# Products with two weight matrices in a graph-transformer kernel: from four matmuls a row tile to Strassen's scheme on pairs of row tiles

## Chip, cores and metric

The kernel runs on one core of one Trainium2 chip. The metric is the device time of one execution in microseconds (us). Times of several runs are given by their median. The profile comes from one further execution, whose own time is given with it.

## What is computed

A layer of graph attention and a layer of graph convolution, in float32, over N = 3327 nodes with D = 512 features. The adjacency `adj` is an N × N matrix; bq and bk are zero vectors in the inputs. Cut to what matters:

```python
h = relu(layernorm(x))
q, k, v = h @ Wq.T + bq, h @ Wk.T + bk, h @ Wv.T + bv
a = q @ k.T / sqrt(D) + adj + adj
x = x + softmax(a) @ v
h = relu(layernorm(x))
A2 = adj + eye(N)
d = diagonal(A2) ** -0.5
temp = A2 @ h @ W.T
x = x + relu((d[:, None] * A2 * d[None, :]) @ temp)
```

Since the rows of the softmax sum to one, softmax(a) @ v is (softmax(a) @ h) @ Wv.T + bv, and the kernel computes it in that order. In the same way temp is (A2 @ h) @ W.T.

## The kernel before

The nodes are padded to 26 row tiles of 128. The work has three stages.

Stage 1 (lines 311 to 374) loads x tile by tile, normalises it (`norm`), makes h with ScalarE, stores h in the buffer `rowd[0]`, and transposes h on TensorE. It also makes M from Wq and Wk and multiplies the transposed h by it. These products use Strassen's scheme in Winograd's form: seven products of half-size blocks in place of eight, with sums and differences of blocks ahead and behind (`Chain`, `four_differences`).

Stage 2 (lines 379 to 563) makes the scores, their exponentials and the sums over the rows, and stores the exponentials in the buffers `pd`.

Stage 3 (lines 574 to 1001) is where the change lies. It has three groups, g = 0, 1 and 2: exponentials times h, A2 times the new h, and A2 times temp. Each group is one big product in Strassen's scheme at two levels. At the outer level there are seven products r, in the order p5, p1, p6, p7, p2, p3, p4. Each is made for two strips of columns, s = 0 (448 columns for each matmul) and s = 1 (384 columns), and each strip in seven steps: t = 0 to 5, and a last, short step t = None. So a group has 98 steps, and `number_of(g, r, s, t)` gives a step's number. In what follows (6,0,1) is the step of product number 6, strip 0, t = 1; a leading 1 in (1,0,0,2) stands for the next group.

A step t = 0 to 5 has seven matmuls (L772), one for each inner product, into seven PSUM banks that keep summing over the strip's steps. The short step has four (L764). The eighth bank, named p8, belongs to the short step's last matmul and, between the short steps, to the products with the weights. For each step:

- `load` issues the DMA of the left side on SyncE's queue, three steps ahead (L751).
- `sums` makes the left side's four sums with three VectorE additions (L170 to L172), two steps ahead.
- `Right.load` and `Right.make` (L715, L731) load the right side's rows and make its eight blocks with VectorE, two to five steps ahead.
- After a short step, `gather` copies p1 out with ScalarE (L806) and combines the eight banks with eight VectorE additions (L807 to L816). `settle` (L795 to L802) then combines outer products. The results are the transposed strips `cts`.
- `Job` (L824 to L842) adds two stored matrices with VectorE and stores the sum with a DMA from GpSimd's queue (POOL in the profile).

When some rows of a group's result are complete in `cts`, the products with the weights begin. They are attached to later steps with `at(k, ...)`, and run after that step's own matmuls. `times_weights` (L844) takes a tile of 128 rows and multiplies it by Wv (g = 0) or W1 (g = 1): four matmuls of 512 columns (L848) into bank p8. For g = 0, `attend_load` (L853) loads the tile of x a step earlier, on ScalarE's queue. `attend` (L857) scales the product by the reciprocal of the softmax sum and adds x (VectorE, L860), adds bv (VectorE, L861), stores the result in `x1d`, and starts the norm. `attended` (L865), a step later, makes the new h with ScalarE (L867) and stores it in `rowd[1]`. For g = 1, `temp` (L872) reads the bank with ScalarE, scaled (L876), and stores the tile in `rowd[2]`. The next group's right sides are loaded from these rows.

The order within each engine is set by hand. `in_order` (L120, L993) keeps VectorE, TensorE, GpSimd, ScalarE and SyncE in the order in which the code writes their instructions. `run(k)` (L973) writes one step: loads, matmuls, gather, sums of step k + 2, settle, and then what `between` holds for k, in the order in which `at` put it there.

Of the kernel before, what the change touches and what calls it, by code (L numbers as in the profile page):

```python
# [15 lines left out]
P = 128  # L16
# [20 lines left out]
PAIRS = 6  # L37
# [7 lines left out]
def graph_layers_kernel(  # L45
# [117 lines left out]
    totd = dram.tile([1, NP], F32, name="totd")  # L163
    x1d = [dram.tile([P, D], F32, name=f"x1d{i}") for i in range(NT)]
# [3 lines left out]
    def four_sums(o, g):  # L168

        nc.vector.tensor_add(o[:, 0:2], g[:, 0:4:3], g[:, 1:2].to_broadcast([P, 2, g.shape[-1]]))  # L170
        nc.vector.tensor_add(o[:, 2], o[:, 1], g[:, 0])  # L171
        nc.vector.tensor_add(o[:, 3], o[:, 2], g[:, 2])  # L172
# [116 lines left out]
    nc.sync.dma_start(bq_sb, bq)  # L289
    M = blocks(range(4, 8), "M")  # L290
# [3 lines left out]
    zero = half(12, [P, P], "zero")  # L294
# [16 lines left out]
    def h_transposed(k):  # L311

        a, n = PACKS[k]
        for _, i in (o for o in order if o[0] == k):
# [9 lines left out]
            if i < HALF:  # L324
                nc.scalar.copy(hp[k][:, 0:2, :, w], pt.rearrange("p (a c) e -> p a c e", a=2))
            else:
                nc.scalar.copy(hp[k][:, 2, :, w], pt[:, 2:4])
                nc.vector.tensor_add(hp[k][:, 3, :, w], hp[k][:, 2, :, w], pt[:, 0:2])
                nc.vector.tensor_add(hp[k][:, 5, :, w], hp[k][:, 0, :, w], pt[:, 0:2])
        nc.vector.tensor_add(hp[k][:, 4], hp[k][:, 3], hp[k][:, 0])  # L330
# [280 lines left out]
    rs = const.tile([P, NT], F32, name="rs")  # L611

    def weights(src):

        w = [half(k, [P, 2, D], "w") for k in (12, 13)]
        for c in range(DC):
            nc.sync.dma_start(w[c // 2][:, c % 2], src[c * P : (c + 1) * P])
        return [w[c // 2][:, c % 2] for c in range(DC)]
# [4 lines left out]
    bvs = []  # L623

    def prepare():
        wv_w1.append(weights(wvT))
        bvs.append(half(11, [P, D], "bv_sb"))
        nc.sync.dma_start(bvs[0], bass.AP(tensor=bv.tensor, offset=bv.offset, ap=[[0, P], [1, D]]))
# [4 lines left out]
    def prepared():  # L633
        nc.vector.reciprocal(rs, tot)
        nc.vector.tensor_scalar(dg, dg, 1.0, None, op0=ALU.add)
        nc.gpsimd.tensor_tensor(sd, dg, mh, op=ALU.pow)

    wv_w1 = []

    def other_weights():  # L640
        wv_w1.append(weights(w1T))
# [17 lines left out]
    r_ring = ring(*((half, k) for k in (4, 5, 6, 7)))  # L659
# [11 lines left out]
    job_ring = ring(*spare[2:], (half, 14))  # L671
    h_ring = ring(*spare[:2])
    ts_ring = ring(*spare[:3])
# [25 lines left out]
    class Right:  # L699
# [31 lines left out]
        def make(self):  # L731
            own, r = self.own, self.r
            if r == "p5":
                nc.vector.tensor_sub(own, self.two[:, :, 0:E], self.two[:, :, E:D])
            if r == "p6":
                nc.vector.tensor_add(own, own, self.two[:, :, 0:E])
                nc.vector.tensor_sub(own, own, self.two[:, :, E:D])
                nc.gpsimd.dma_start(self.t2[:, 0 : 2 * self.n], self.b[:, 0 : 2 * self.n])
            if r in ("p7", "p4"):
                nc.vector.tensor_sub(own, own, self.one)  # L740
            if self.n == 2:
                for _ in four_differences([self.b[:, k] for k in range(8)]):
                    pass

    class Step:
# [8 lines left out]
        def sums(self):  # L754
# [3 lines left out]
            four_sums(self.o, self.a.rearrange("p k y w -> p (k y) w"))  # L758

        def multiply(self, ps):  # L760
            a, b, w = self.a, self.right.b, Q[self.s]
            if self.t is None:
                for k, (y, z) in enumerate(((0, 0), (0, 1), (1, 0), (1, 1))):
                    nc.tensor.matmul(ps[("p2", "p3", "p4", "p8")[k]][:, :w], b[:, z], a[:, 0, y],  # L764
                                     start=k == 3, stop=True)
                return
            o = self.o
            for r, i, m in (
# [3 lines left out]
                nc.tensor.matmul(ps[r][:, :w], b[:, i], m, start=self.t == 0,  # L772
                                 stop=self.t == PAIRS - 1 and r in ("p1", "p5", "p6", "p7"))
# [70 lines left out]
    def times_weights(i, w):  # L844
        s, y, k = where(i)
        ps = bank(ROLE["p8"], "p8")
        for d in range(DC):
            nc.tensor.matmul(ps, cts[s][y][d][:, k * P : (k + 1) * P], w[d], start=d == 0, stop=d == DC - 1)  # L848
        return ps

    xts = {}

    def attend_load(i):  # L853
# [525 lines left out]
```

## Time and profile before

| what | value |
|---|---|
| median of three runs | 2237.49 us (2237.46 to 2239.75) |
| the profiled execution | 2234.41 us |
| its span in the profile | 2232.6 us, so 1.8 us lie around it |
| mean granted clock of TensorE | 0.993 |
| TensorE (PE) busy | 2183.9 us |
| VectorE (DVE) busy | 1622.8 us |
| ScalarE (ACT) busy | 230.8 us |
| GpSimd (POOL) busy | 357.0 us |
| products with Wv and W1, L848 | 125.4 us (x272) and 67.6 us (x144) |

In the profile PE is TensorE's matmuls and PEld its weight loads, which overlap them. A line such as `L848 PE MATMUL p<-w,ct 128*128 128x512 f32 x272 | 125.4, 601` is a group of instructions: line 848, the engine, the operation, output and inputs with their shapes, the number of records, and after the bar the busy time in us and the mean length of one in ns. What follows a second bar is the idle time of the engine just before them and what ended most of it. Matmuls overlap, so the mean length of one (601 ns here) is more than the distance from one to the next; busy time counts overlaps once. A float32 matmul leaves two records: `x416` for L848, in its two groups, are 208 matmuls, four for each of 26 tiles in two groups g. A wait line gives the instruction that waited, the one that released it, the total in us, how often, and the longest.

### The profile page before, as it was taken

The numbers are of one execution on the slowest core, as the hardware profiler recorded it, in microseconds if no ns is written. First come the engines' busy times: TensorE is split into PE (matmuls) and PEld (weight loads), VectorE is DVE, ScalarE is ACT, GpSimd is POOL, SyncE is SP. The second block draws the span as 40 slices with busy tenths as digits, with TensorE's granted clock in tenths as the row PEclk, the third lists the DMA queues.
The fourth block names the chain that finished last, engine by engine and source line by source line (L and its number), as shares of the span: only waits on it lengthen the run. The fifth ranks groups of instructions, "written<-read, shape, count | busy, mean of one in ns | idle before, by whom it ended". The sixth has DMA issues, their size and how long they took to land. (4 is left out here: it accounts for less than half of the span.)

```text
span 2232.6 us, 21006 instructions
## 1 busy us (share of the span) xinstructions
PE 2183.9 (98%) x6268; PEld 1166.9 (52%) x6268; DVE 1622.8 (73%) x3096; ACT 230.8 (10%) x336; POOL 357.0 (16%) x555
## 2 busy tenths in 40 slices
PE   9999999999999999999999999999999999999996
PEld 6555555455555555555444555555554555555554
DVE  6369888788777788877777778886543457777775
ACT  5321121112110000000010000000000000000011
POOL 4223333333321000001222110000000000000001
PEclk9999999999999999999999999999999999999998
DMA  7568888888969898888787899876636458766684
GB/s 249 203 218 301 297 293 286 303 285 303 355 205 335 318 362 295 283 297 275 254 299 238 300 341 354 279 277 199 223 119 203 141 176 291 247 196 190 212 304 151
DMA packets 246412, 583.68 MB, mean 261 GB/s; under 512 B 34770, under 2 KB 105904, under 8 KB 246288
## 3 DMA queue, kind: packets, MB, share of 16 engines
q1 hardware_dynamic: 191824, 398.89, 53.9%
q0 software_dynamic: 45104, 167.88, 19.9%
q10 hardware_dynamic: 9360, 15.47, 2.2%
q8 instruction: 52, 0.85, 0.2%
q14 instruction: 72, 0.59, 0.1%
HBM read 414.28 MB, written 167.85 MB: 261 GB/s over the span
## 5 line engine op out<-in xcount | busy, mean ns | idle before, releaser
L772 PE MATMUL p<-part,b 128*128 128x448 f32 (+1 forms) x3528 | 1253.2, 513 | 5.8 <-DVE part L171 5.2
L772 PEld LDWEIGHTS p<-part,b 128*128 128x128 f32 x3528 | 666.7, 190 | 572.6 <-issue 297.9
L170 DVE TENSOR_TENSOR part<-part 128x896 f32<-128x896 f32 (+1 forms) x252 | 256.6, 1018 | 84.9 <-PE p L772 40.1
L449 PE MATMUL Y<-qt,hp 128*128 128x448 f32 (+1 forms) x832 | 309.3, 514 | 4.6 <-DVE g L453 3.6
L449 PEld LDWEIGHTS Y<-qt,hp 128*128 128x128 f32 x832 | 157.1, 190 | 140.7 <-issue 72.3
L449 PE MATMUL Z<-qt,hp 128*128 128x384 f32 (+1 forms) x416 | 162.6, 513 | 0.0
L172 DVE TENSOR_TENSOR part<-part,part 128x448 f32<-128x448 f32 (+1 forms) x219 | 129.4, 591 | 16.7 <-PE p L772 0.9
L171 DVE TENSOR_TENSOR part<-part,part 128x448 f32<-128x448 f32 (+1 forms) x219 | 129.4, 591 | 7.3
L848 PE MATMUL p<-w,ct 128*128 128x512 f32 x272 | 125.4, 601 | 5.7 <-DVE part L860 4.0
L764 PE MATMUL p<-part,b 128*128 128x448 f32 (+1 forms) x336 | 124.2, 513 | 0.0
L449 PEld LDWEIGHTS Z<-qt,hp 128*128 128x128 f32 x416 | 78.8, 190 | 67.4 <-issue 36.4
L453 DVE SCALAR_TENSOR_TENSOR g<-g,Y 128x384 f32<-128x384 f32 (+1 forms) x156 | 91.3, 585 | 26.9 <-PE Y L449 25.4
L842 POOL DMA_DIRECT2D sum<-job x52 | 28.4, 547 | 486.8 <-DVE job L839 267.7
L807 DVE TENSOR_TENSOR part<-p,part 128x384 f32<-128x384 f32 (+1 forms) x33 | 19.3, 585 | 105.7 <-ACT part L806 57.5
L764 PEld LDWEIGHTS p<-part,b 128*128 128x128 f32 x336 | 63.5, 190 | 53.7 <-issue 32.8
L848 PEld LDWEIGHTS p<-w,ct 128*128 128x128 f32 x272 | 51.9, 192 | 67.5 <-issue 51.9
L806 ACT COPY part<-p 128x384 f32<-128x384 f32 (+1 forms) x33 | 16.5, 499 | 667.4 <-PE p L772 667.4
L449 PE MATMUL X<-qt,hp 128*128 128x384 f32 (+1 forms) x208 | 81.1, 513 | 0.0
L456 ACT ACTIVATE g<-g 128x768 f32<-128x768 f32 (+1 forms) x48 | 43.0, 896 | 353.8 <-DVE g L453 291.9
L848 PE MATMUL p<-w,part 128*128 128x512 f32 x144 | 67.6, 606 | 5.5 <-DVE ct L816 5.5
L441 POOL DMA_DIRECT2D sum<-o x52 | 36.8, 709 | 222.2 <-DVE o L435 155.7
L89 POOL DMA_DIRECT2D out_dram<-r x34 | 18.4, 542 | 302.9 <-DVE r L897 275.0
(160 smaller groups left out, 1877.8 us busy)
## 6 DMA issues: line engine op xcount, KB each, us to landing
part<-sum SPq DMA_DIRECT2D x104, 448.0 KB, 4.9
part<-p SPq DMA_DIRECT2D x91, 448.0 KB, 6.6
part<-sum SPq DMA_DIRECT2D x104, 384.0 KB, 3.5
part<-p SPq DMA_DIRECT2D x91, 384.0 KB, 4.0
part<-in_adjT_dram SPq DMA_DIRECT2D x78, 448.0 KB, 4.9
b<-row SPq DMA_DIRECT2D x234, 128.0 KB, 4.9
part<-in_adjT_dram SPq DMA_DIRECT2D x78, 384.0 KB, 3.7
g<-in_adjT_dram SPq DMA_DIRECT2D x52, 448.0 KB, 4.7
```

What stands on the lines that cost most here:

```text
L170: nc.vector.tensor_add(o[:, 0:2], g[:, 0:4:3], g[:, 1:2].to_broadcast([P, 2, g.shape[-1]]))
L171: nc.vector.tensor_add(o[:, 2], o[:, 1], g[:, 0])
L172: nc.vector.tensor_add(o[:, 3], o[:, 2], g[:, 2])
L441: nc.gpsimd.dma_start(self.to(sumd)[:, 0:2], self.o)
L449: nc.tensor.matmul(ps[:, :wd], h_of(self.t, name, k), qt[B[name]][:, k], start=start and k == 0, stop=k == 1, skip_group_check=True)
L453: nc.vector.scalar_tensor_tensor(a[n], a[n], 2.0, ps[:, :wd], op0=ALU.mult, op1=ALU.add if sign > 0 else ALU.subtract)
L456: nc.scalar.activation(g[1], g[1], AF.Exp, **({"bias": pad} if self.t == HALF - 1 else {}))
L764: nc.tensor.matmul(ps[("p2", "p3", "p4", "p8")[k]][:, :w], b[:, z], a[:, 0, y], start=k == 3, stop=True)
L772: nc.tensor.matmul(ps[r][:, :w], b[:, i], m, start=self.t == 0, stop=self.t == PAIRS - 1 and r in ("p1", "p5", "p6", "p7"))
L807: nc.vector.tensor_sub(c22, p["p6"], c11)
L842: nc.gpsimd.dma_start(sumd[self.s][self.j][:, 2 + self.k], self.a)
L848: nc.tensor.matmul(ps, cts[s][y][d][:, k * P : (k + 1) * P], w[d], start=d == 0, stop=d == DC - 1)
```

## The change

The products with Wv and W1 are now made for pairs of row tiles, 13 pairs in each of the two groups g. A pair is a matrix of 2 × 2 blocks of 128 rows by 256 columns, and the weight matrix is 2 × 2 blocks of 256 × 256. `Weighted` makes the seven products of Strassen's scheme in the order p2, m1, p5, p6, p3, p7, p4 (`PARTS`). Each part has two matmuls of 256 columns, into one or the other half of bank p8, where successive parts are partly summed. After each part its half is read, scaled, by ScalarE (p2, p5, p6, p4) or by VectorE, which adds to what is there (m1, p3, p7).

A pair belongs to one step k. In that step a part is followed by one of the step's seven matmuls (by two between p7 and p4). After each of these, two operations of `beside` are written: the sums of step k + 2 and then all that `between` holds for k. For this, `four_sums`, `make` and `multiply` became generators. Eight VectorE additions of 128 × 128 blocks, which a pair needs, are written at the end of step k − 1 (`coming`).

For g = 0, x + bv is made in stage 1 with one VectorE addition for each tile, and stored by a DMA from GpSimd's queue in the new buffer `xbd`. At the end of step k an accumulating DMA adds it to the tile in place of the load of x and of the two additions (`close`). The store in `x1d` and the norm follow in step k + 1, and the relu and the store in `rowd[1]` in step k + 2. The weights are loaded as blocks into four half slots, and their four differences and a change of sign are made in later steps. Some buffers move: the ring for right-side rows has three slots and not four, the ring for jobs has four other slots, bv lies in slot 12 from stage 1 on.

Line numbers of the changed kernel are those of its own file: the block additions are at L879, the parts' matmuls at L889, ScalarE's read at L899, VectorE's at L901, the accumulating DMA at L917.

The diff, cut to its core:

```diff
@@ -327,6 +330,8 @@
                 nc.scalar.copy(hp[k][:, 2, :, w], pt[:, 2:4])
                 nc.vector.tensor_add(hp[k][:, 3, :, w], hp[k][:, 2, :, w], pt[:, 0:2])
                 nc.vector.tensor_add(hp[k][:, 5, :, w], hp[k][:, 0, :, w], pt[:, 0:2])
+            nc.vector.tensor_add(xt, xt, bv_sb)
+            nc.gpsimd.dma_start(xbd[i], xt)
         nc.vector.tensor_add(hp[k][:, 4], hp[k][:, 3], hp[k][:, 0])
         nc.vector.tensor_add(hp[k][:, 6], hp[k][:, 1], hp[k][:, 4])
...
@@ -609,36 +614,45 @@
     def weights(src):
 
-        w = [half(k, [P, 2, D], "w") for k in (12, 13)]
-        for c in range(DC):
-            nc.sync.dma_start(w[c // 2][:, c % 2], src[c * P : (c + 1) * P])
-        return [w[c // 2][:, c % 2] for c in range(DC)]
+        if not W:
+            b11, b21, b22, t1, t2, t3, t4, b12 = blocks((7, 12, 13, 14), "w")
+            W.extend((b11, b12, b21, b22, t1, t2, t3, t4))
+        for z in range(2):
+            for y in range(2):
+                block = src[z * E : (z + 1) * E, y * E : (y + 1) * E]
+                nc.sync.dma_start(W[2 * z + y], block.rearrange("(c p) e -> p c e", p=P))
+        differences.append(four_differences(W))
+
+    differences = []
+
+    def difference():
+        next(differences[-1])
+
+    def turn_sign():
+        nc.scalar.mul(W[0], W[0], -1.0)
 
...
     b_ring = ring(*((half, k) for k in (0, 1, 2, 3, 8, 9, 10)))
-    r_ring = ring(*((half, k) for k in (4, 5, 6, 7)))
+    r_ring = ring(*((half, k) for k in (4, 5, 6)))
...
     spare = [(mid, k) for k in range(10, 15)]
-    job_ring = ring(*spare[2:], (half, 14))
-    h_ring = ring(*spare[:2])
-    ts_ring = ring(*spare[:3])
+    job_ring = ring(*spare[1:])
+    ts_ring = ring(*spare)
...
-    def times_weights(i, w):
-        s, y, k = where(i)
-        ps = bank(ROLE["p8"], "p8")
-        for d in range(DC):
-            nc.tensor.matmul(ps, cts[s][y][d][:, k * P : (k + 1) * P], w[d], start=d == 0, stop=d == DC - 1)
-        return ps
-    xts = {}
-    def attend_load(i):
-        xts[i] = view(2, 1).rearrange("p a w -> p (a w)")[:, len(xts) % 3 * D :][:, :D]
-        nc.scalar.dma_start(xts[i], x[i * P : (i + 1) * P])
-    def attend(i):
-        xt, ps = xts[i], times_weights(i, wv_w1[0])
-        nc.vector.scalar_tensor_tensor(xt, ps, rs[:, i : i + 1], xt, op0=ALU.mult, op1=ALU.add)
-        nc.vector.tensor_add(xt, xt, bvs[0])
-        nc.gpsimd.dma_start(x1d[i], xt)
-        normed[i] = norm(xt)
-    def attended(i):
-        h1 = h_ring([P, D], "h1")
-        nc.scalar.activation(h1, xts[i], AF.Relu, bias=normed[i][1](), scale=normed[i][0])
-        nc.gpsimd.dma_start(rowd[1][i], h1)
-    normed = {}
-    def temp(i):
-        ps = times_weights(i, wv_w1[1])
-        ts = ts_ring([P, D], "ts")
-        nc.scalar.mul(ts, ps, sd[:, i : i + 1])
-        nc.gpsimd.dma_start(rowd[2][i], ts)
+    PARTS = (("p2", 1, True, 0, 1), ("m1", 0, True, 0, -1), ("p5", 1, False, 3, -1), ("p6", 0, False, 1, -1),
+             ("p3", 1, False, 1, 1), ("p7", 0, False, 3, 1), ("p4", 0, False, 2, 1))
+    class Weighted:
+        def __init__(self, *its):
+            self.its = its
+        def sums(self):
+            a11, a12, a21, a22 = self.blocks = [
+                [cts[s][y][2 * z + c][:, k * P : (k + 1) * P] for c in range(2)]
+                for s, y, k in map(where, self.its) for z in range(2)
+            ]
+            self.o = half(11, [P, 4, 2, P], "rows")
+            for k, x, y in ((1, a21, a22), (2, None, a11), (3, None, a12), (0, a11, a21)):
+                for c in range(2):
+                    yield nc.vector.tensor_add(self.o[:, k, c], self.o[:, {2: 1, 3: 2}[k], c] if x is None else x[c], y[c])
+        def start(self):
+            self.ps = bank(ROLE["p8"], "pw").rearrange("p (k e) -> p k e", k=2)
+        def multiply(self, j):
+            name, k, new, _, _ = PARTS[j]
+            left = {"m1": 0, "p2": 1, "p4": 3}.get(name)
+            for c in range(2):
+                a = self.o[:, {"p7": 0, "p5": 1, "p6": 2, "p3": 3}[name], c] if left is None else self.blocks[left][c]
+                nc.tensor.matmul(self.ps[:, k], a, W[B[name]][:, c], start=new and c == 0, stop=c == 1,
+                                 skip_group_check=True)
+        def read(self, j):
+            name, k, _, n, sign = PARTS[j]
+            i = self.its[n // 2]
+            to, ps = self.to[n // 2][:, n % 2 * E : (n % 2 + 1) * E], self.ps[:, k]
+            scale = self.scales[sign][:, i : i + 1]
+            if name in ("p2", "p5", "p6", "p4"):
+                nc.scalar.mul(to, ps, scale)
+            else:
+                nc.vector.scalar_tensor_tensor(to, ps, scale, to, op0=ALU.mult, op1=ALU.add)
+    class Attended(Weighted):
+        scales = {1: rs, -1: nrs}
+        places = itertools.cycle(((0, 1), (2, 3)))
+        def start(self):
+            super().start()
+            v = view(2, 1).rearrange("p a w -> p (a w)")
+            places = [*(v[:, n * D : (n + 1) * D] for n in range(3)), W[1].rearrange("p a e -> p (a e)")]
+            self.to = [places[n] for n in next(Attended.places)]
+        def close(self):
+            for i, xt in zip(self.its, self.to):
+                nc.gpsimd.dma_start(xt, xbd[i], accum_op=ALU.add)
+        def norm(self):
+            self.normed = []
+            for i, xt in zip(self.its, self.to):
+                nc.gpsimd.dma_start(x1d[i], xt)
+                self.normed.append(norm(xt))
+        def then(self):
+            for i, xt, (rstd, bias) in zip(self.its, self.to, self.normed):
+                nc.scalar.activation(xt, xt, AF.Relu, bias=bias(), scale=rstd)
+                nc.gpsimd.dma_start(rowd[1][i], xt)
+    class Temp(Weighted):
+        scales = {1: sd, -1: nsd}
+        def start(self):
+            super().start()
+            self.to = [ts_ring([P, D], "ts") for _ in self.its]
+        def close(self):
+            for i, ts in zip(self.its, self.to):
+                nc.gpsimd.dma_start(rowd[2][i], ts)
...
+    weighted, coming = {}, {}
+    def rows(k, i, *z):
+        at(k - 1, finish_load, i, *z)
+        at(k, finish, i, *z)
+    def pair(g, k, *its):
+        w = weighted[k] = (Attended, Temp)[g](*its)
+        coming.setdefault(k - 1, []).append((w.sums, ()))
         if g == 0:
-            at(k - 1, attend_load, i)
-            at(k, attend, i)
-            at(k + 1, attended, i)
-        elif g == 1:
-            at(k, temp, i)
-        else:
-            at(k - 1, finish_load, i, *z)
-            at(k, finish, i, *z)
-    for g in range(3):
-        for t, i in {2: 0, 3: 1, 4: 2, 5: 3}.items():
-            rows(g, number_of(g, 5, 1, t), i)
-        for t, i in enumerate((4, 5, 6, 14, 15, 16)):
-            rows(g, number_of(g, 6, 0, t), i)
-        for t, its in {1: (7,), 2: (8, 9), 3: (10,), 4: (11, 12), 5: (13,)}.items():
-            for i in its:
-                rows(g, number_of(g, 6, 1, t), i)
-        if g < 2:
-            for k, i in enumerate((*range(20, 26), *range(17, 20))):
-                rows(g, number_of(g + 1, 0, 0, 0) + 2 * k, i)
+            at(k + 1, w.norm)
+            at(k + 2, w.then)
+    for g in range(2):
+        for (n, r, s, t), its in {
+            (0, 5, 1, 2): (0, 1), (0, 5, 1, 4): (2, 3),
+            (0, 6, 0, 1): (4, 5), (0, 6, 0, 3): (6, 14), (0, 6, 0, 5): (15, 16),
+            (0, 6, 1, 2): (7, 8), (0, 6, 1, 3): (9, 10), (0, 6, 1, 5): (11, 12),
+            (1, 0, 0, 2): (13, 19), (1, 0, 0, 4): (20, 21),
+            (1, 0, 1, 1): (22, 23), (1, 0, 1, 3): (24, 25), (1, 0, 1, 5): (17, 18),
+        }.items():
+            pair(g, number_of(g + n, r, s, t), *its)
...
-    at(number_of(1, 1, 0, 4), other_weights)
+    at(number_of(1, 1, 0, 4), weights, w1T)
+    for k in (number_of(0, 1, 0, 0), number_of(1, 2, 0, 0)):
+        for n in range(4):
+            at(k + n, difference)
+        at(k + 4, turn_sign)
...
+    def flow(tasks):
+        for what, args in tasks:
+            yield from what(*args) or (None,)
     def run(k):
         step = steps[k]
@@ -980,14 +1062,32 @@
             set_up()
         if step.t is None:
             banks_of["p8"] = bank(ROLE["p8"], "p8")
-        step.multiply(banks_of)
-        rest = gather(cts[step.s], step.r, step.s, banks_of) if step.t is None else None
-        if k + 2 < len(steps):
-            steps[k + 2].sums()
-        if rest:
-            rest()
-        for what, args in between.get(k, ()):
-            what(*args)
+        w = weighted.get(k)
+        sums = steps[k + 2].sums() if k + 2 < len(steps) else iter(())
+        others = between.get(k, ())
+        if w is None:
+            for _ in step.multiply(banks_of):
+                pass
+            rest = gather(cts[step.s], step.r, step.s, banks_of) if step.t is None else None
+            for _ in sums:
+                pass
+            if rest:
+                rest()
+            for _ in flow((*others, *coming.get(k, ()))):
+                pass
+            return
+        beside = itertools.chain(sums, flow(others))
+        w.start()
+        for j, _ in enumerate(itertools.chain((None,), step.multiply(banks_of))):
+            if j != len(PARTS) - 1:
+                w.multiply(min(j, len(PARTS) - 1))
+                w.read(min(j, len(PARTS) - 1))
+            for _ in itertools.islice(beside, 2):
+                pass
+        for _ in itertools.chain(beside, flow(coming.get(k, ()))):
+            pass
+        w.close()
```

## The prediction

> **What bounds the kernel now.** I read the page's busy times first, then TensorE's waits, then the chain of work that ended last, then the timeline and the windows around the products with Wv and W1.
>
> ```profile
> span 2232.6 us, 21006 instructions
> ...
> PE 2183.9 (98%) x6268; PEld 1166.9 (52%) x6268; DVE 1622.8 (73%) x3096; ACT 230.8 (10%) x336; POOL 357.0 (16%) x555
> ```
>
> TensorE is busy for 98% of the span; VectorE has 610 us free in the mean, ScalarE almost everything. So streaming taken from TensorE is time, and every wait put on TensorE is time.
>
> ```profile
> PE p L848 <- DVE ct L816: 5.5, 2, 4.8
> ...
> PE p L848 <- DVE part L860: 4.0, 3, 2.3
> ...
> PE p L848 <- ACT ts L876: 1.7, 2, 0.8
> ```
>
> The old products (L848) wait 11.2 us in seven places (total, times, longest). From the chain (start, duration), long undisturbed stretches of step matmuls:
>
> ```profile
> 1301.39 27.09 PE p L772 x84
> ...
> 1331.06 31.57 PE p L772 x84
> ```
>
> A matmul leaves two records. 27.09/84 = 0.3225 us a record at 384 columns, 31.57/84 = 0.3758 at 448: 0.833 ns a column and 2.5 ns. That gives 0.429 at 512 and 0.2158 at 256: 0.858 us for an old 512-column matmul, 0.432 for a new 256-column one, 0.645 and 0.752 for a step matmul of strip 1 and 0.
>
> **What the Trainium skill says.** "TensorE: Matmul & The Clock Gate", Back-to-back issue gap: N columns take N/2.4 GHz and about 2.5 ns; the two lengths above agree, with two passes a record. The same page, Part 1: an idle window of about 3.4 us halves TensorE's clock, and about 3.4 us of work restores it; the windows below agree. "PSUM — Partial Sum Buffer", Terms: two engines may not be in one bank at once; in the trace a product that reuses its bank starts only after the read. "DMA: Bandwidth & Descriptors", SWDGE vs HWDGE: an accumulating DMA can be issued by GpSimd only; this trace has none.
>
> **The change, part by part.**
>
> *Streaming.* A pair of row tiles took 8 × 0.858 = 6.87 us and takes 7 × 2 × 0.432 = 6.04. 26 pairs in two groups: **−21.4 us**. A weight load lasts 190 ns (page, L772), under the 216 ns of a record, so loads stay hidden.
>
> *Old waits.* The 11.2 us go, with about 0.1 of refill each: −12. A long wait costs more than itself (timeline, then windows whose first column after the interval is length and whose column before the last two is the clock):
>
> ```profile
> 1063.97 5.36 PE L848 MATMUL p<-w,ct 128*128 128x512 f32 x8 [2.31 <-DVE part L860]
> ```
> ```profile
> 1064.00:1065.00 1.00, 1.00 (x2) 0.48 (x3) 0.97 (x2) 0.00 (x0) 0.06 (x1) 0.50 1.02 410
> ...
> 1068.00:1069.00 1.00, 1.00 (x4) 0.45 (x3) 0.96 (x3) 0.00 (x0) 0.00 (x0) 1.00 0.33 132
> ```
>
> After 2.31 us idle the clock is 0.50 for some 3.4 us and eight records take 5.36 us, where the same eight took 3.60 elsewhere: 1.75 us more. The same befalls the 4.78 us wait at 1214.19. Both go: −3.5. Another 2 us are small waits of step matmuls in these steps, which my walk below counts anew: −2.
>
> *Turnaround in the bank.* All seven parts of a pair use one bank (its two halves in turn), and in the built program each part's first matmul waits for the read of the part before. Between parts stands one step matmul. What a turnaround takes, from the two places where the old kernel reused the bank at once:
>
> ```profile
> 1124.69 3.60 PE L848 MATMUL p<-w,ct 128*128 128x512 f32 x8
> ...
> 1128.33 0.75 DVE L860 SCALAR_TENSOR_TENSOR part<-p,rs,part 128x512 f32<-128x512 f32 x1 [2.11 <-PE p L848]
> ...
> 1129.13 2.41 PE L848 MATMUL p<-w,ct 128*128 128x512 f32 x5 [0.84 <-DVE part L860]
> ```
>
> Streaming ends at 1124.69 + 8 × 0.429 = 1128.12; 0.21 until the read, the read 0.75, 0.05 to the next matmul, 0.10 of refill. With ScalarE (L876 at 1700.33) it is 0.26 + 0.69 + 0.05 + 0.10. For 256 columns ScalarE's scaled read takes 0.473 (L896), VectorE's about 0.475 (L328 0.412, plus the 0.06 by which L860 exceeds L861). So 0.88 with ScalarE and 0.835 with VectorE, against one step matmul of 0.752 or 0.645: a wait of 0.13/0.08 in strip 0, 0.24/0.19 in strip 1. A pair has three such ScalarE and two such VectorE waits (p7 to p4 has two step matmuls between): 0.55 or 1.10 us. Five and eight pairs a group: 11.6; both groups: **+23**. Bounds: 15 to 30.
>
> *VectorE late at its reads.* This is the largest term. m1 is read by VectorE, in written order behind everything that the step before left there: sums of two steps on, a job, the making of right sides, the norm, eight new adds of blocks (L879; 0.22 pitch, 1.8 us), and two operations of this step. p5 waits for that read. Formerly one read a tile came after the product's end and TensorE went on with the step; now TensorE waits in the middle of it. After a gather VectorE lags, as the kernel before shows:
>
> ```profile
> 1044.72 2.74 PE L764 MATMUL p<-part,b 128*128 128x384 f32 x8
> ...
> 1061.17 0.95 DVE L839 TENSOR_TENSOR job<-job 128x768 f32<-128x768 f32 x1
> ```
>
> VectorE ends the work of step (6,0,0) at 1062.1, 17.4 us after the short step's start. (I name steps by product number, strip, t; a leading 1 is the next group's first product.) In the new kernel its gather starts some 1 us earlier, since no read stands ahead; then the block adds 1.8 and two operations of (6,0,1) 1.75: m1's read at about +20.1. TensorE gets there at 2.7 + 5.26 + p2 0.86 + step matmul 0.75 + m1 0.86 = +10.4, and would wait for the read's end with its turnaround from +11.2 on: about **9.5 us**. The same walk, with sums 2.3/2.1, a right side 1.66, a job 1.0, norms 2.04 a pair, gather 3.9 to 4.2 and settle 1.8 to 2.05, gives in the first group: (5,1,2) 1.4; (5,1,4) 1.7; (6,0,1) 9.5; (6,0,3) 2.6; (6,0,5) 2.6; (6,1,2) 6.1; (6,1,3) 0.9; (6,1,5) 2.5; (1,0,0,2) 9.8; (1,0,0,4) 2.05; then 3.9, 2.8, 2.5: **+48**. The second group has no norms and few jobs: 0.8, 6.3, 3.3, 0.9, 6.6, 1.1: **+19**. I bound the two at 45 and 90 together. Some eight of these waits exceed 2.3 us in a way that halves the clock: 8 × 1.75 = 14, **+13** with overlaps (bounds 7 and 18).
>
> *x + bv.* The x load (ScalarE's queue, 26) and the bv add (0.69 each on VectorE, not on the path) go; the accumulating DMA (L917) comes, on POOL, two a pair. Its row is absent: plain 256 KB transfers of POOL's queue land in 3.0 (row<-ts) to 5.3 us (row<-h); I take 4.4 (x1d<-part), and it is in the walk, as the norm on VectorE and POOL's later stores wait for it. At 3.0 the first group loses 8 us less; at 10, 40 more. On POOL's queue the 26 new issues of 0.54 (14 us over some 160) stand ahead of the norm's power, the stores of x1d and row, which move one step later, and a job's store. Who waits for these is the norm, and a load several steps on; POOL is busy for 46 of the 203 us from 1017 to 1220, so I add nothing, at most 5 if a row's reload comes before its store has landed.
>
> *Stage 1.* 26 adds of 0.69 (18 us of VectorE) and 26 POOL issues of 0.54 to 0.57 (14.5). In the first 110 us TensorE is busy for 103.6 and VectorE for 55, so VectorE's slack hides them; without it, 6. I take **+2**. The load of bv goes to ScalarE's queue there, once. The weights' differences (eight VectorE operations of 0.69 and two sign turns) stand in steps without pairs, and VectorE makes its sums two steps ahead: 0, at most 3. The ring for right-side rows loses a slot (4 to 3), so a load may start one use later; loads are issued three to five steps, 14 us and more, ahead of use and land in 5 to 6: 0, at most 5.
>
> *Sum.* −21.4 − 12 − 3.5 − 2 + 23 + 48 + 19 + 13 + 2 = +66. The profiled execution took 2234.4 us (span 2232.6 and 1.8 around it), 3.1 under the median of the runs: 2300 for it, **2303** for the median.
>
> **The rivals.**
>
> *A: VectorE is in time.* If it catches up before its reads, the 80 us of lateness and half clock go: −38.9 + 23 + 2 = −14, 2224; with the turnaround hidden as well, 2200. It speaks for it that VectorE's load over 1017 to 1220 us (146 of 203) hardly grows: 23 + 18.5 of block adds and reads against 37.4 removed. Against it: the lag after a gather is measured, 17 us, while TensorE comes in 10. It decides faster or slower at about a fifth of the lateness that I count. Chance 0.12.
>
> *B: a small part of the lateness.* A third to a half of it, 27 to 40 us, gives 2251 to 2264; at a fifth, no change. Chance of within 0.2%: 0.03; of 2242 to 2255: 0.05.
>
> *C: the accumulating DMA is slow*, 10 us: VectorE holds at the norm with all reads behind it, 2343. Against it: 256 KB lands in 3 to 5.3 us on every queue here. Chance 0.08.
>
> *D: it doesn't do what it says:* 256-column matmuls at the pace of the weight loads. 190 ns against 216 excludes it unless the loads are held up.
>
> **How the numbers follow.** The sum has 0.72. With its bounds taken all at once it spans 2266 to 2343, and 2258 with the accumulating DMA at 3.0. Leaving out A, the unchanged case and half of C leaves 0.19 outside: 2242 to 2345. What this measurement can tell from no change is about 0.2%, 4.5 us. Faster 0.12, same 0.03, slower 0.85.
>
> **What would show it.** TensorE's waits should name the reads: some 80 us on VectorE's (L901) and about 10 on ScalarE's (L899), the longest at (6,0,1) and the third step of each next group; new matmul records of 216 ns; TensorE busy down by some 20 us apart from half clock; clock at 0.98 or less. Wrong would be waits on L901 under 30 us in all, or parts that start before the last read has ended.

## The result and the profile after

| | before | after |
|---|---|---|
| median | 2237.47 us (4 runs) | 2307.55 us (4 runs) |
| the profiled execution | 2234.41 us | 2308.75 us |
| its span | 2232.6 us | 2307.0 us |
| TensorE's mean granted clock | 0.993 | 0.985 |

The changed kernel takes 1.033 times as long, with a 95% interval from 1.0304 to 1.0356. The prediction was 2303 us, slower, with a range from 2242 to 2345.

The page of the changed kernel, its first lines and the largest group of the new matmuls (after the second bar: TensorE's idle time just before them, and what ended most of it):

```profile
span 2307.0 us, 22140 instructions
...
PE 2203.3 (96%) x6580; PEld 1226.4 (53%) x6580; DVE 1679.1 (73%) x3365; ACT 262.9 (11%) x417; POOL 385.2 (17%) x607
...
L889 PE MATMUL pw<-w,rows 128*128 128x256 f32 x416 | 125.7, 428 | 45.1 <-DVE part L901 29.2
```

TensorE was to be relieved, yet its busy time rose by 19 us, and its share of the span fell from 98 to 96%. TensorE's waits in the changed kernel (total, times, longest):

```profile
PE pw L889 <- DVE part L901: 29.2, 11, 4.1
PE pw L889 <- ACT part L899: 15.7, 6, 4.7
PE pw L889 <- DVE ts L901: 13.0, 6, 5.4
...
PE pw L889 <- ACT w L899: 2.8, 2, 2.2
```

The old lines of L848 were 11.2 us. In their place stand 61.3 us (with one small line of 0.6 us): 42.2 on VectorE's reads and 19.1 on ScalarE's.

To see where the span grew, I compared the starts of the short steps (L764 before, L776 after) in both timelines. The changed kernel reaches the first short step of stage 3 4.7 us later. Then it runs level, but for 1.7 us in product 3 (the clock, shown in the part on the prediction), until the pairs begin. In the first group the stretch from the short step of product 5, strip 0, to that of the next group's product 1, strip 0, grew from 297.33 us to 350.10; in the second group from 285.18 to 303.21. With small shifts in the last group and the tail (−2.8) the sum is 74.4. The busy columns of these windows split both growths (first number: length; then each engine's busy time). Before:

```profile
1000.89:1298.22 297.33, 288.28 (x762) 144.43 (x761) 215.89 (x429) 23.51 (x32) 62.44 (x92) 0.99 0.80 275
1557.65:1842.83 285.18, 282.81 (x761) 144.17 (x760) 139.78 (x266) 20.45 (x32) 14.03 (x26) 1.00 0.55 171
```

After:

```profile
1007.29:1357.39 350.10, 299.15 (x917) 176.60 (x916) 215.64 (x520) 46.30 (x84) 76.93 (x118) 0.96 0.74 232
1616.84:1920.05 303.21, 287.63 (x917) 170.80 (x916) 177.05 (x409) 27.37 (x58) 14.04 (x26) 0.98 0.52 161
```

First group: TensorE is busy 10.9 us longer and idle 41.9 us longer. Second group: 4.8 and 13.2. VectorE's load in the first group did not grow at all (215.9 and 215.6). So its throughput isn't what costs; when it comes to its reads is.

The worst place is (6,0,1), one of the two that the prediction named, but it has two waits in a row. Here is its timeline in the changed kernel (start, duration, engine, line; in brackets the idle time before and its releaser):

```profile
1068.82 0.22 DVE L201 SCALAR_TENSOR_TENSOR nb<-mv,rstd 128x1 f32<-128x1 f32 x2
...
1069.01 0.81 ACT L927 ACTIVATE part<-part,nb,rstd 128x512 f32<-128x512 f32 x1 [16.93 <-DVE nb L201]
1069.72 0.80 ACT L927 ACTIVATE w<-w,nb,rstd 128x512 f32<-128x512 f32 x1
...
1070.43 0.45 ACT L899 ACTIVATE part<-pw,rs 128x256 f32<-128x256 f32 x1
...
1070.94 1.70 PE L889 MATMUL pw<-w,ct 128*128 128x256 f32 x4 [4.67 <-ACT part L899]
...
1075.01 0.49 DVE L879 TENSOR_TENSOR rows<-ct 128x128 f32<-128x128 f32 x2
1075.41 1.09 DVE L171 TENSOR_TENSOR part<-part 128x896 f32<-128x896 f32 x1
1076.54 0.62 DVE L172 TENSOR_TENSOR part<-part,part 128x448 f32<-128x448 f32 x1
1077.08 0.48 DVE L901 SCALAR_TENSOR_TENSOR part<-pw,nrs,part 128x256 f32<-128x256 f32 x1
...
1077.61 1.55 PE L889 MATMUL pw<-w,rows 128*128 128x256 f32 x4 [3.48 <-DVE part L901]
```

VectorE makes the bias of the pair before (L201) only after the gather of the short step, its sums, its settling and its right side. ScalarE's relu (L927) waits for that, and p2's read stands behind the relu. So m1 waits 4.67 us for ScalarE, and p5 then 3.48 us for VectorE: 8.15 together, where I had 9.5 for VectorE alone. The four records at 1070.94 take 1.70 us, and 0.86 undisturbed: in the trace the clock is 0.50 from 1071.36 to 1074.78.

Where nothing is late, the turnaround is seen alone. From the changed kernel's chain, a pair in strip 1 (start, duration):

```profile
1858.16 0.86 PE pw L889 x4
1859.03 0.65 PE p L784 x2
1859.67 1.10 PE pw L889 x4
1860.77 0.65 PE p L784 x2
1861.42 1.12 PE pw L889 x4
...
1867.70 1.29 PE p L784 x4
1868.99 0.86 PE pw L889 x4
```

A part takes 0.86 us when its bank is free, and 1.05 to 1.13 when one step matmul alone stands between it and the part before.

### The profile page after: what moved, and what is told of

The parts are those of the page before. It is cut to its first block, busy times and chain, and to the rows that moved or that the text cites. A ratio compares the mean times of both kernels' runs of the same rounds, so it can differ in the third digit from the quotient of the medians.

```text
span 2307.0 us, 22140 instructions
## 1 busy us (share of the span) xinstructions
PE 2203.3 (96%) x6580; PEld 1226.4 (53%) x6580; DVE 1679.1 (73%) x3365; ACT 262.9 (11%) x417; POOL 385.2 (17%) x607
## 5 line engine op out<-in xcount | busy, mean ns | idle before, releaser
L784 PE MATMUL p<-part,b 128*128 128x448 f32 (+1 forms) x3528 | 1286.0, 516 | 10.7 <-DVE part L172 5.3
L889 PE MATMUL pw<-w,rows 128*128 128x256 f32 x416 | 125.7, 428 | 45.1 <-DVE part L901 29.2
L889 PEld LDWEIGHTS pw<-w,rows 128*128 128x128 f32 x416 | 77.3, 204 | 115.3 <-DVE part L901 46.4
L776 PE MATMUL p<-part,b 128*128 128x448 f32 (+1 forms) x336 | 124.2, 513 | 0.0
L776 PEld LDWEIGHTS p<-part,b 128*128 128x128 f32 x336 | 63.5, 190 | 50.7 <-issue 29.4
L889 PE MATMUL pw<-w,ct 128*128 128x256 f32 x192 | 53.1, 400 | 14.5 <-ACT part L899 13.4
L941 POOL DMA_DIRECT2D row<-ts x26 | 14.0, 540 | 306.6 <-DVE ts L901 262.5
```

The source lines that it names most:

```text
L776: yield nc.tensor.matmul(ps[("p2", "p3", "p4", "p8")[k]][:, :w], b[:, z], a[:, 0, y], start=k == 3, stop=True)
L784: yield nc.tensor.matmul(ps[r][:, :w], b[:, i], m, start=self.t == 0, stop=self.t == PAIRS - 1 and r in ("p1", "p5", "p6", "p7"))
L889: nc.tensor.matmul(self.ps[:, k], a, W[B[name]][:, c], start=new and c == 0, stop=c == 1, skip_group_check=True)
```

## The experiments

Each is timed beside the kernel before on the same chip. The ratio is to that kernel and is given with its 95% interval. The edits are cut to their core. They are made to the changed kernel; that of x + bv alone is made to the kernel before.

### The second group alone

```diff
-    for g in range(2):
+    for g in (1,):
         for (n, r, s, t), its in {
...
+    def old_rows(k, i):
+        at(k - 1, attend_load, i)
+        at(k, attend, i)
+        at(k + 1, attended, i)
```

> Strassen's products on pairs for W1 (g = 1) alone; the first group keeps its four matmuls a tile, the load of x and the addition of bv. In the profile of the changed kernel the second group is 18.0 us longer than before, and the first group 52.8. My theory (VectorE and ScalarE come late to a read that TensorE waits for, and most so in the first group, which has the norms, the relus and the jobs): 2237.5 + 18 = 2255, between 2250 and 2262. The rival that the cost lies in the scheme itself, a fixed price for each pair (turnaround in the bank, clock): half of the 70 us, 2272.

2259.85 us, ratio 1.0102 (1.0086 to 1.0119). Within the expected span, and not at the 2272 of the rival, an equal price for each pair. In its profile the second group grows by 19.9 us. The first group grows by 6.9 us, though its products are the old ones: one wait of a product for a gather is 7.6 us there, and 4.8 in the kernel before. The buffers that had to move for the weights may be the reason; no run tests it. What follows: a pair in the first group costs more than twice what it costs in the second.

### x + bv alone

```diff
-        nc.vector.scalar_tensor_tensor(xt, ps, rs[:, i : i + 1], xt, op0=ALU.mult, op1=ALU.add)
-        nc.vector.tensor_add(xt, xt, bvs[0])
-        nc.gpsimd.dma_start(x1d[i], xt)
+        nc.scalar.mul(xt, ps, rs[:, i : i + 1])
+        nc.gpsimd.dma_start(xt, xbd[i], accum_op=ALU.add)
+
+    def attend_norm(i):
+        xt = xts[i]
+        nc.gpsimd.dma_start(x1d[i], xt)
         normed[i] = norm(xt)
```

> The old products of four matmuls a tile, but x + bv made in stage 1 and added by the accumulating DMA, with the norm a step later and the relu two steps later, as in the change. My theory: the DMA itself costs little; stage 1 costs the 4.7 us by which the changed kernel reaches the first short step later, and the first group is at most some 8 us longer, as VectorE waits at the norm but TensorE waits for no read in the middle of a step: 2245, between 2238 and 2256. The rival that the accumulating DMA and the norm behind it alone make the first group's 35 us more than the second's: 2270 or more.

2240.63 us, ratio 1.002 (1.0008 to 1.0033): 4 us with stage 1 included, within the expected span. VectorE's norm waits for the accumulating DMA in this kernel far longer than in the changed one, where the lines are 28.1 and 11.7 us:

```profile
DVE st L191 <- DMA part<-xb: 73.4, 15, 8.5
```

With 31.4 us more for the tiles in another buffer that is over 100 us, in a kernel that is 4 us longer in all. The edit also gives the read of the bank to ScalarE, so no read that TensorE waits for stands behind VectorE's wait.

### The relu behind the reads

```diff
-            at(k + 2, w.then)
+            coming.setdefault(k + 2, []).append((w.then, ()))
```

> The changed kernel with the relu of a pair written at the end of step k + 2, behind that step's reads on ScalarE, and not ahead of them. TensorE's waits name ScalarE's reads for 18.5 us in the profile of the changed kernel, since a relu that waits for VectorE stands ahead of p2's read. My theory says that VectorE's lateness is behind both, and that m1's read by VectorE comes at the same time as before in most of these places: 2303, between 2297 and 2307. The rival that ScalarE's queue is a cost of its own: the 18.5 us and some half clock go, 2285.

2345.54 us, ratio 1.0481 (1.0462 to 1.0501): 38 us slower than the changed kernel. Both expectations missed. The waits of VectorE's norm on the accumulating DMA rose from 39.8 to 68.5 us:

```profile
DVE st L191 <- DMA part<-xb: 59.8, 14, 10.2
...
DVE st L191 <- DMA w<-xb: 8.7, 5, 2.1
```

On GpSimd's queue the relu's stores in `rowd[1]` stand ahead of the accumulating DMAs of the pair in step k + 2, in the changed kernel too. A relu behind the reads ends later, and its stores, which wait for it, now hold those DMAs back: in seven of the 13 pairs the first of them is issued within 0.3 us of such a store's end, against three in the changed kernel. The next run tells this apart from a cost of the relu's place.

### The same, with the accumulating DMAs first

```diff
-        for _ in itertools.chain(beside, flow(coming.get(k, ()))):
+        for _ in beside:
             pass
         w.close()
+        for _ in flow(coming.get(k, ())):
+            pass
```

> As the run with the late relu, but with the pair's accumulating DMAs written ahead of the relu and its stores on GpSimd's queue. In that run VectorE's norm waited 68 us for the accumulating DMA, against 40 in the changed kernel. If those DMAs came late because a store that waits for a relu stood ahead of them on the queue: VectorE waits 40 us or less again, and the time is 2300, between 2285 and 2312. If the late relu itself costs (places that come free later): 2335 or more.

2315.05 us, ratio 1.0358 (1.0334 to 1.0381). VectorE's wait is 45.1 us, and some 30 of the 38 us are back. It is 3 us above the span that I gave. So stores that wait, ahead of other DMAs on GpSimd's queue, were most of the loss.

That the relu's new place gains nothing doesn't clear the relu. TensorE waits longest for ScalarE at the first pair after a short step, for p2's read: 4.7, 4.5, 2.8 and 1.8 us in the changed kernel, 13.8 of the 18.5 in the first group. There the relu that stands ahead of the read was written two steps earlier, in a step that has no pair, so this edit leaves it ahead. The waits are still 4.7, 4.0, 1.5 and 1.8.

### All reads by ScalarE

```diff
-                nc.vector.scalar_tensor_tensor(to, ps, scale, to, op0=ALU.mult, op1=ALU.add)
+                term = self.terms[:, len(self.later) * E :][:, :E]
+                nc.scalar.mul(term, ps, scale)
+                self.later.append((to, term))
```

> The changed kernel with all seven reads of the bank by ScalarE; what VectorE added from the bank (m1, p3, p7) goes to a buffer of three terms, and VectorE adds it from there at the end of its step, with TensorE waiting for none of it. My theory: the 42 us of waits for VectorE's reads shrink to what the block additions, which p5 needs, are late themselves; about 1.75 us of sums and 0.5 us of read fall away at each of some 17 waits: 2275, between 2262 and 2290. The rival that the waits come from the one bank's turnaround whoever reads: 2302 to 2312.

2272.38 us, ratio 1.016 (1.0143 to 1.0177): half of the loss is gone, as expected. TensorE's waits of this kernel:

```profile
PE pw L890 <- ACT part L900: 22.7, 8, 4.7
...
PE pw L890 <- ACT w L900: 4.2, 2, 3.7
...
PE pw L890 <- DVE rows L879: 3.2, 5, 2.1
```

The 42.2 us on VectorE's reads are gone; 3.2 come back on the block additions and 9.1 more on ScalarE (two lines of 0.7 and 0.6 us included), whose queue still holds the relus. The second group is now only 2.7 us longer than before the change, the first 30.6. VectorE still adds the same terms, only later. What was taken away is TensorE's wait for it.

### Two parts a gap

```diff
-            if j != len(PARTS) - 1:
-                w.multiply(min(j, len(PARTS) - 1))
-                w.read(min(j, len(PARTS) - 1))
+            two = {0: (0, 1), 2: (2, 3), 4: (4, 5), 6: (6,)}.get(j, ())
+            for n in two:
+                w.multiply(n)
+            for n in two:
+                w.read(n)
```

> As the run with all reads by ScalarE, but two parts stand one behind the other, then their two reads, then two of the step's matmuls: three turnarounds a pair, each beside two matmuls (1.29 or 1.50 us), in place of five that one matmul (0.65 or 0.75) doesn't hide. My prediction put 23 us on the turnaround. If that holds, some 20 of them go: 2252, between 2246 and 2260. If the turnaround costs nothing to speak of, 2268 or more.

This kernel keeps the reads by ScalarE. 2250.26 us, ratio 1.0068 (1.0049 to 1.0088): 22.1 us less than the run before, and the prediction's turnaround was 23. In the profiles 19.0 us of this lie in the two groups' stretches; the rest is stage 1 and the clock elsewhere. The second group is now 7.2 us shorter than in the kernel before the change.

### Leaving out the norm, or the accumulating DMA

The first of these kernels leaves out the second layer norm (statistics, power and bias), the second the addition of x + bv. Both give other values than the layer; only their time is used.

```diff
-                self.normed.append(norm(xt))
+                self.normed.append(None)
```

> The changed kernel without the second layer norm: of the statistics, the power on GpSimd and the bias nothing is left, the relu is taken of the attended rows as they are (its place, its stores and the accumulating DMA stay). If the first group's 35 us more than the second's come from VectorE's norm, its wait for the accumulating DMA, and the relu that waits for VectorE: 2307.5 - 35 = 2272, between 2262 and 2285. If they come from the jobs and from stores and places: 2295 or more.

2281.39 us, ratio 1.021 (1.0193 to 1.0227): 26 us less than the changed kernel, of the 35 by which its first group grew more than its second. The accumulating DMA still runs here; what is gone is VectorE's wait for it, and VectorE's work on the norm.

```diff
-                nc.gpsimd.dma_start(xt, xbd[i], accum_op=ALU.add)
+                pass
```

> The changed kernel without the accumulating DMA: x + bv is still made and stored in stage 1, but not added, and the norm, the relu and the stores work on the scaled product alone. In the profile of the changed kernel VectorE's norm waits 40 us for that DMA, with the reads behind it. If that wait is passed on to TensorE in half of its length, with the half clock: 2287, between 2275 and 2297. If VectorE would have waited for the reads anyway: 2300 or more.

2278.24 us, ratio 1.0184 (1.0167 to 1.0201): 29 us less than the changed kernel, more than I expected. TensorE's longest waits at the pairs in this kernel:

```profile
PE pw L889 <- DVE ts L901: 12.7, 5, 5.4
PE pw L889 <- DVE part L901: 10.2, 6, 3.1
PE pw L889 <- ACT part L899: 9.7, 5, 3.4
```

The first group's (part, and 0.6 us on w) fell from 47.7 us to 20.5, while those of the second (ts) stay. The same DMA cost at most 4 us in the run with x + bv alone. In these runs it costs where a read that TensorE needs is queued behind VectorE's wait for it.

### Everything together, twice

Reads by ScalarE, two parts a gap, accumulating DMAs first, norm a step later, relu behind the reads:

> All together: reads by ScalarE alone, two parts a gap, accumulating DMAs first, norm two steps behind the pair so that VectorE doesn't wait for the DMA, relu behind the reads. My theory: what stays is the gain of 21 us of streaming and of some 15 us of the old waits, less 5 in stage 1 and some 15 of waits for late block additions after the short steps: 2222, between 2210 and 2238. The rival that VectorE's total load sets the time: 2245 or more.

2252.89 us, ratio 1.0081 (1.0062 to 1.0101). Missed by 30 us, and no better than two parts a gap. VectorE's norm waits for the DMA for 6.5 us, against 51.4 with two parts a gap. But TensorE's waits for ScalarE's reads into the buffer of terms rose from 6.2 us to 24.6, as ScalarE itself waits ahead of its reads:

```profile
PE pw L890 <- ACT terms L903: 24.6, 6, 7.8
...
ACT part L934 <- DMA x1d<-part: 43.1, 5, 16.2
ACT part L934 <- DVE nb L201: 41.5, 3, 16.1
...
ACT part L900 <- DMA row<-part: 14.3, 3, 7.0
```

The relu writes in place, so it waits for the store of x1d to have read the tile. This wait was not new: the changed kernel has 34.2 us of it, and the wait at (6,1,2) is one of these. In the second version that store is issued ahead of the norm, pairs and relus are set apart, and the block additions of pairs next to a short step are made up to three steps ahead:

```diff
-            at(k + 2, w.norm)
-            coming.setdefault(k + 2, []).append((w.then, ()))
+            at(k + 1, w.store)
+            at(k + n, w.norm)
+            coming.setdefault(k + r, []).append((w.then, ()))
```

> The run before with everything together missed its 2222 by 30 us; its profile names three waits that I had not costed: the relu in place waits on ScalarE for the store of x1d, issued in the same step, with the next reads behind it; reads wait for a row's store to free the place of the pair before last; relus of pairs next to a short step wait for a late VectorE. Here the store of x1d is issued a step ahead of the norm, those relus stand a step or two later, pairs stand four steps apart where they share a place, and the block additions of pairs behind a short step are made up to three steps ahead. The waits on ScalarE's and VectorE's lines at the pairs' matmuls were 30 us there; if two thirds and half of the half clock go: 2230, between 2220 and 2240. If there are yet other waits: 2245 or more.

2244.18 us, ratio 1.004 (1.0026 to 1.0054). Missed again. The x1d waits are gone, but another grew, and TensorE waits for ScalarE nearly as long:

```profile
PE pw L890 <- ACT terms L903: 20.1, 6, 6.7
...
ACT part L900 <- DMA row<-part: 37.3, 5, 8.7
```

There are four places for the tiles of two pairs, and a read into a place now waits until the row's store has left it. I have no run with more places; that this alone is left in the first group is not shown.

### The second group alone, with both remedies

The first run's kernel, with reads by ScalarE and two parts a gap:

> The first group as in the kernel before (without the change's buffers for x + bv), the second with Strassen's products, reads by ScalarE alone and two parts a gap. In the run with two parts in both groups the second group is 7.2 us shorter than in the kernel before; in the run with the second group alone it was 19.9 us longer and the rest of the kernel 9.5 longer by other buffers. Theory: 2236.5 + 7.4 - 7.2 + 1 = 2238, between 2230 and 2244, 20 or more under the 2260 of the second group alone. The rival that the gain seen in the second group depends on the first: 2248 or more.

2230.2 us, ratio 0.9976 (0.9967 to 0.9985; 14 runs), 8 us under what I expected and at the lower edge of the span: faster than both kernels, if by 0.24% against the kernel before only. In its profile the second group is 7.1 us shorter than before the change; the first, with the old products, is 6.7 longer, as in the other run of this kind. In its timeline a pair in strip 1:

```profile
1697.36 1.89 PE L897 MATMUL pw<-w,ct 128*128 128x256 f32 x8
1699.09 1.45 PE L791 MATMUL p<-part,b 128*128 128x384 f32 x4
1700.38 1.89 PE L897 MATMUL pw<-w,rows 128*128 128x256 f32 x8
```

From start to start, two parts take 1.73 us (8 records of 0.216), and the two step matmuls 1.29, their undisturbed time. The turnaround is hidden.

## Why the prediction was right

The forecast and what the profiles of the two kernels show, in us:

| term | forecast | in the profiles |
|---|---|---|
| streaming | −21.4 | −21.4, at 0.86 a part |
| old waits, small waits of step matmuls | −12 − 2 | −11.4 |
| turnaround | +23 | +22.3, what is left of the busy time (below) |
| lateness at the reads, first and second group | +48, +19 | +47.7, +13.6 |
| other late work of VectorE in these stretches | 0 | +5.2 |
| half clock, new less old | +9.5 | +14.8, and +3.4 elsewhere |
| stage 1 | +2 | +4.7 |
| last group and tail | 0 | −4.5 |
| sum | +66 | +74.4 (by the medians +70.1) |

The mechanism, waits for late reads in the middle of a step, was right, and so was its size in the first group. That the total came within 5 us is partly luck: the second group's lateness was put too high, the clock, stage 1 and VectorE's other work too low.

*Streaming.* Right. An undisturbed part takes 0.86 us, four records of 0.215, in the chain above; no weight load held it up.

*Small waits of step matmuls.* They are not there. In the two stretches TensorE was idle for 11.4 us before the change, and 11.2 of them were the old products'.

*Turnaround.* Right. In the pair of the chain the five shortened gaps cost 0.24 + 0.26 + 0.19 + 0.19 + 0.27 = 1.15 us, where I had 1.10. The single ones are off: I had 0.24 behind ScalarE and 0.19 behind VectorE, and those behind VectorE are the 0.26 and 0.27. Two parts a gap took 19.0 us away in the two groups' stretches.

*Lateness.* Right for the first group, and mostly by place: (6,0,1) 8.2 us for 9.5, (6,1,2) 4.5 for 6.1, (1,0,0,2) 6.9 for 9.8, the longest of the walk; but (1,0,0,4) 5.1 for 2.05. What I had wrong is who is waited for: I expected some 80 us on VectorE's reads and 10 on ScalarE's, and the waits list 42.2 and 19.1. The prediction didn't name the relu. At the first pair after a short step it stands ahead of p2's read, and waits for VectorE's bias, or at (6,1,2) for the store of x1d, which its in-place write must follow. The run with ScalarE's reads confirms the mechanism for VectorE's part. That the rest comes from the relu is read from the traces; no run takes only the relu away. The 5.2 us of other late work, above all two right sides made 2.0 us late (L747), had no term.

*Half clock.* Put too low. In the stretches at clock 0.50 TensorE is busy for 28.7 us in the first group and 7.6 in the second, against 6.7 and 0 before the change. Half of that is lost: 11.0 and 3.8 us more. What is then left of the growth of TensorE's busy time, with 10.7 us of streaming less in each group, is the turnaround, as it shows in longer records and not in idle time: 10.9 + 10.7 − 11.0 = 10.6 and 4.8 + 10.7 − 3.8 = 11.7. So one sign that I gave, TensorE busy for some 20 us less apart from half clock, could not appear; and the clock was 0.985 in the profiled execution, where I had 0.98 or less.

The length of a wait alone doesn't tell: after 2.24 us idle at 1098.76 four records took 2.07 us, after 2.83 at 1212.13 they took 1.13. The traces show what does. In each trace the starts of the stretches at 0.50 lie whole multiples of 3.41 us apart, so the clock goes by intervals of a fixed grid. Take TensorE's idle time in every such interval of the 13 traces, from 36 us on. Of the intervals at full clock, none with under 1.77 us of idle time was followed by one at half clock, and all 96 with over 2.01 us were. Of the 2.24 us, 2.15 lie in one interval; the 2.83 are cut into 2.01 and 0.82. The prediction said that its windows agree with an idle window of about 3.4 us; here some 2 us of it are enough. One wait of 1.93 us is in both kernels, until 884.72 before the change and until 889.42 after it. Two intervals before:

```profile
883.02:886.43 3.41, 1.71 (x5) 1.06 (x6) 3.31 (x6) 0.00 (x0) 0.54 (x1) 1.00 0.57 192
886.43:889.85 3.42, 3.42 (x12) 2.08 (x11) 3.18 (x6) 0.00 (x0) 0.00 (x0) 1.00 0.78 241
```

After:

```profile
887.05:890.46 3.41, 1.48 (x5) 0.68 (x4) 3.34 (x5) 0.00 (x0) 0.54 (x1) 1.00 0.56 207
890.46:893.87 3.41, 3.41 (x7) 1.81 (x6) 3.13 (x6) 0.00 (x0) 0.00 (x0) 0.50 0.56 173
```

Before, the grid cuts off 0.23 us of the wait and leaves 1.70 in the interval shown. After, one interval holds all of it, and the next runs at half clock: the 1.7 us in product 3. What a wait of this length costs is thus in part luck of where it falls.

*Stage 1.* Put too low. 4.7 us is one execution. Over the ten traces of kernels with x + bv in stage 1 the first short step starts at 678.1 to 683.9 us (median 681.8), over the three without it at 673.4 to 676.8 (median 674.5). That is some 7 us, over the 6 that I gave as the bound; the kernel with x + bv alone was 4 us longer in all.

*The accumulating DMA.* It lands in 4.9 us (part<-xb) and 6.0 (w<-xb) by the median, where I took 4.4. (Plain transfers of 256 KB took up to 5.8 us in the kernel before, rows<-row on SyncE's queue, not up to 5.3 as I had read.) Rival C was wrong on its price of 10 us. But I treated its 4.4 us as one term among many. Leaving it out saves 29 us in this schedule, more than any other single piece left out; leaving out the norm, which takes the same wait of VectorE away, saves 26. It is a cause only in company: alone it cost at most 4.

*Rival A*, VectorE in time, is where the experiments lead: with TensorE waiting neither for VectorE's reads nor for the turnaround, the second group is 7.2 us shorter, of a possible 10.7 + 2.4. In the first group no run got there.

## What to carry to other kernels

Before splitting a product into parts that share one accumulator bank, count the reads that the next part must wait for, and ask of each engine that makes such a read what is queued ahead of it, a DMA that it waits for included. Give such reads to an engine whose queue holds nothing that waits, and do the additions later from SBUF. Two parts ahead of one gap with two other matmuls hide a turnaround that one matmul doesn't.

## What the runs showed that I had not expected

- A wait of VectorE for a DMA of over 100 us in all cost at most 4 us, and one of 40 us cost 29, by what was queued behind it.
- With the late relu, writing two accumulating DMAs a pair ahead of two stores that wait for it, on GpSimd's queue, saved 30 us of 2346.
- One and the same wait of 1.93 us cost 1.7 us of half clock in one kernel and none in another, by where it fell in the 3.41 us intervals of the clock.
